# A graph network on one core: the attention's first gathers wait for older TensorE steps, and the last early chunk comes in two halves

## The chip, the cores and the metric

The kernel runs on one core of a Trainium2 chip. The time is device microseconds of one execution, given as the median of several executions; a program on one core has no other core to wait for. The five engines of the core (TensorE or PE, VectorE or DVE, ScalarE or ACT, GpSimd or POOL, SyncE or SP) run their own instruction streams and meet only at semaphores. DMAs are issued here by SP (plain loads and stores) and by POOL (gathers, which read rows of a table in device memory by a list of indices).

## The reference, cut to what matters

Node features are normalised, go through two message-passing convolutions over 200,000 edges and an attention over the same edges, and are added to the input. There are 6,250 nodes of 128 features; edges are sorted by destination.

```python
def mesh_conv(x, src, dst, ea, w1, b1, g, bt, w2, b2):
    m = concatenate([x[dst], x[src], ea], axis=-1) @ w1 + b1
    m = silu(group_norm(m, g, bt))
    m = m @ w2 + b2
    out = segment_sum(m, dst, num_segments=n)
    cnt = segment_sum(ones, dst, num_segments=n)
    return out / clip(cnt, 1.0)[:, None]

h = relu(layernorm(x))                                  # h0
h = silu(group_norm(mesh_conv(h, ...c1), n1_g, n1_b))
h = h + (silu(t_emb) @ tm_w + tm_b)
h = silu(group_norm(mesh_conv(h, ...c2), n2_g, n2_b)) + h0
q, k, v = h @ qw + qb, h @ kw + kb, h @ vw + vb         # 8 heads of 16
logits = (q[dst] * k[src]).sum(-1) * scale + (edge_attr @ ew + eb)
pe = exp(logits - segment_max(logits, dst)[dst])
w = pe / clip(segment_sum(pe, dst)[dst], 1e-06)
o = segment_sum(w[:, :, None] * v[src], dst) @ ow + ob
out = x + h + group_norm(o, an_g, an_b)
```

## The kernel before

**Chunks.** The edges are cut into 1,563 tiles of 128, and 8 tiles make a chunk (`TPC = 8`), so that there are 196 chunks (`NCH`). Chunk number c stands for j = 195 - c: the list is walked from its end. The last chunk, c = 195, has only 3 tiles. Each of three stages (convolution 1, convolution 2, attention) walks all 196 chunks.

**Gathers.** For each tile of a chunk one indirect DMA on POOL (L796, in `gather`) fetches the 128 rows that the edges' sources name: from `b_d` (128 numbers a row) in a convolution, from `kv_d` (k and v, 256 numbers a row) in the attention. The destination's part of the message needs no gather: it is a matmul of a one-hot matrix `ohT` with a window `pk` of a table (L1252 in a convolution, L1521 `qe` in the attention; this matmul is the chunk's "product"). Every gather is ordered behind the one before it (`follows`, `kept.behind`), so POOL runs them in one line: chunk 0, 1, 2, ... of one stage, then of the next.

**Early chunks.** A table is complete only when the stage before it has worked out its last node tile. So that POOL need not stand still there, the first three chunks of convolution 2 and of the attention (`EARLY = 3`) are gathered while the stage before still runs, from copies of the tables, `b_e` and `kv_e`, in which the rows of that last tile are zero. What is missing is added later by a matmul of a one-hot `ohS` with the last tile's rows, `late` (in the attention: `complete`, L1700 and L1702). From chunk 3 on the full tables are read. In the last steps of a stage `pipeline` calls `following.prefetch(c)` for c = 0, 1, 2 of the next stage.

**Buffers.** The gathered rows of chunk c stand in buffer c mod 4 in a convolution and in c mod 11 (`G + 3`) in the attention: `ge0` to `ge2` for the early chunks, `g3` to `g9`, and `gl`. The buffers g3 to g9 use memory that the convolutions had.

**Steps.** `pipeline` (L896 on) is one loop over steps n for each stage. In the attention, step n fetches chunk n + 2 (loads on SP, gathers on POOL); then, where chunks are due, adds up weighted values of older chunks (`second`, L1602); then the logits of chunk n (`first`, L1536 to L1542); in the steps that end a run, the running maxima over the run (`maxima`: two transposes on PE and two scans on DVE, L1565 to L1581); then the one-hot of chunk n + 2 on ACT (`compared`, L763 and L764) and, last, the product of chunk n + 1 on PE. Runs are 4 chunks first (0 to 3), then 8 (4 to 11, 12 to 19, ...), and at the end shorter. Chunks 0 to 3 are weighted and summed in steps 5 to 8, chunks 4 to 11 in steps 13 to 20; steps 9 to 12 have no such work. A chunk's buffer is free when its values have been weighted (`weighted`, L1595), which is done at the end of the step before its sums. On DVE, ACT, PE and SP the instructions run in the order in which the program issues them (`in_order`); POOL's gathers keep their own line.

**The hold.** Before the fetch in step n, `kept.seen` is set to the name of the last PE instruction issued so far (`last_product`), and the first gather of the chunk gets a dependency on it (`held`). In the attention that is mostly the product of chunk n, so the gathers of chunk c may not start before the product of chunk c - 2 is done. The first fetch in the loop of a stage is free of it (`fetched`); in the attention that fetch is chunk 2's, which has its gathers already, and in convolution 1 it is chunk 2's as well. Prefetches of the next stage are held in the same way. `go_on` issues pieces of the node work (batches of four node tiles, once their edges are all summed), which have PE instructions of their own; `last_product` can name one of these.

**The end of a stage.** After the loop `flush` adds the last sums, and `last_tile` (L1187 on) works through the last node tile, with `nodes_of` as a generator: in convolution 2 it stores k and v of that tile into `kv_d` (L1080) and a copy of the node features into `h2_d` (L1105).

Of the kernel before, what the change touches and what calls it, by code (L numbers as in the profile page):

```python
# [31 lines left out]
TPC = 8  # L32
# [6 lines left out]
EARLY = 3  # L39
# [18 lines left out]
def kernel(ctx: ExitStack, tc: tile.TileContext, x, src, dst, eat, w, out):  # L58
# [12 lines left out]
    NCH = -(-EI // TPC)  # L71
# [16 lines left out]
    kept = SimpleNamespace(h0=hpc.tile([P, NW, D], FP, name="h0"))  # L88
# [80 lines left out]
    b_d = {i: dram.tile([NW * P, D], FP, name=f"b_d{i}") for i in (1, 2)}  # L169
    kv_d = dram.tile([NW * P, KV], FP, name="kv_d")  # L170
    b_e = dram.tile([NW * P, D], FP, name="b_e")
    kv_e = dram.tile([NW * P, KV], FP, name="kv_e")
# [72 lines left out]
    with tc.tile_pool(name="node0", bufs=1) as np_, tc.tile_pool(name="prep", bufs=1) as pp, \  # L245
# [99 lines left out]
        back, firsts = sums[:, :NCH], sums[:, 2 * P:2 * P + NCH]  # L345
# [79 lines left out]
    def steps_of(i):  # L425


        ends, due, n = {}, {}, 0
        for m in spread(i):
            ends[n + m] = list(range(n, n + m))  # L430
            due.setdefault(n + m + (i == 3 or n < NCH - SOON), []).extend(ends[n + m])
            n += m
        waiting, todo, left = [], [], NCH
        while left:
            n = len(todo)
            waiting += due.get(n, ())
            steps = min([m for m in due if m > n], default=n + 1) - n
            k = -(-len(waiting) // steps)
            todo.append(waiting[:k])
            waiting = waiting[k:]  # L440
            left -= k
        return ends, todo
# [318 lines left out]
    def compared(k):  # L761

        nc.scalar.activation(k.ohT[:WN, :], k.rel, AF.Square, bias=minus_p[:WN])  # L763
        nc.scalar.activation(k.ohT[:WN, :], k.ohT[:WN, :], AF.Relu, bias=1.0, scale=-4.0)  # L764
# [26 lines left out]
            tc.add_to_no_dep_group(key, h.ins)  # L791

    def gather(k, g, table_d, ring=None):
        n = k.nt
        for t in range(n):
            h = nc.gpsimd.indirect_dma_start(  # L796
                out=g[:, t, :table_d.shape[1]], out_offset=None, in_=table_d,
                in_offset=bass.IndirectOffsetOnAxis(ap=k.src[:, t:t + 1], axis=0))
            if ring is None:
                continue  # L800
            if kept.behind is not None:
                follows(h, kept.behind)
            kept.behind = h.ins
            if t == 0 and kept.seen is not None:
                held(h, kept.seen)
            ring.mark(h, k.at, t, n - 1)

    kept.behind = kept.seen = None

    def last_product():  # L810
        return next((i.name for i in reversed(nc.cur_bb.bb.instructions) if i.engine == mybir.EngineType.PE), None)

    def held(h, name):
        tc.add_manual_dep(
            h.ins, name, mybir.DependencyInfo(mybir.DependencyClass.Sync, mybir.DependencyReason.DATA),
            reason="held until TensorE is there")

    def follows(h, behind):
        tc.add_manual_dep(
            h.ins, behind.name,  # L820
            mybir.DependencyInfo(mybir.DependencyClass.NoSync, mybir.DependencyReason.DATA),
            reason="behind the gathers")
        return h
# [69 lines left out]
    def pipeline(i, stage, following=None, aside=iter(()), then=iter(())):  # L893


        ends, todo = steps_of(i)  # L896
        starts = {n: j for j, (n, _, _) in enumerate(plans[i])}
        ahead = stage.ahead
        ks, under_way, said, fetched = stage.ks, [], {}, False

        def go_on(n, those):
            for g in those:
                if said.get(g) == "held" and n + 1 in ends:
                    continue
                said[g] = next(g, STOP)
                if said[g] is STOP:
                    under_way.remove(g)

        for c in range(ahead):
            if c not in ks:  # L910
                ks[c] = stage.fetch(c)
                compared(ks[c])
        stage.products(ks[0])
        for n, seconds in enumerate(todo):
            new = None
            if n + ahead < NCH and n + ahead not in ks:
                kept.seen = last_product() if fetched else None
                new = ks[n + ahead] = stage.fetch(n + ahead)
                kept.seen, fetched = None, True
            elif following and n + ahead >= NCH:  # L920
                kept.seen = last_product()
                new = following.prefetch(n + ahead - NCH)
                kept.seen = None
            if n + 1 < NCH and stage.soon:
                stage.products(ks[n + 1])
            run = [ks[c] for c in ends.get(n, ())]
            stage.root(run)
            early = stage.soon and n > NCH - SOON
            if early:
                ahead_of = [g for g in under_way if said.get(g) not in ("var", "root")]  # L930
                go_on(n, ahead_of)
            if new and stage.soon:
                compared(new)
            first = (lambda k: lambda: stage.first(k))(ks[n]) if n < NCH else None
            stage.then = [ks[c] for c in (todo[n + 1] if n + 1 < len(todo) else ()) if c in ks]
            if stage.second(run, [ks.pop(c) for c in seconds], first) and first:
                first()
            stage.finish()
            if new and not stage.soon:
                compared(new)  # L940
            if n + 1 < NCH and not stage.soon:
                stage.products(ks[n + 1])
            if n + 1 < len(todo):
                stage.early(ks, n, todo[n + 1])
            if n in starts:
                for _ in aside:
                    pass
                under_way.append(stage.batch(starts[n]))
            go_on(n, [g for g in under_way if not early or g not in ahead_of])
            if n > 4 and next(aside, STOP) is STOP and n > min(starts):  # L950
                next(then, None)
            if n < NCH:
                stage.reduce(ks[n])
        stage.flush()
        for g in (*under_way, aside, then):
            for _ in g:
                pass
# [206 lines left out]
    def nodes_of(b, i, w, m, hx=None):  # L1164
        return attention_nodes(b, w, m, hx) if i == 3 else conv_nodes(b, i, w, m, last=hx is not None)
# [22 lines left out]
    def last_tile(b, i, hx=True):  # L1188

        slots, b.bank = b.bank(), None  # L1190
        turn = itertools.cycle(range(BN))

        def slot():
            j = next(turn)
            return slots[:, j:j + 1, :]

        b.bank = slot
        b.var = lambda: last_var
        b.rs = last_rs
        nc.scalar.activation(last_sd[:, :1], eps_t, AF.Sqrt)  # L1200
        for r in nodes_of(b, i, 0, 1, hx):
            if r == "root":
                nc.scalar.activation(last_sd, last_var, AF.Sqrt, bias=eps_t, scale=1.0 / HD)  # L1203
            if r == ("inverse" if i == 3 else "root"):
                nc.vector.reciprocal(last_rs, last_sd)  # L1205
# [10 lines left out]
    def convs(general=False):  # L1216
        with ExitStack() as es:
            pool = lambda n, b, **kw: es.enter_context(tc.tile_pool(name=f"{n}{'g' if general else 'c'}", bufs=b, **kw))
            pools = {"oh": pool("oh", 2), "ps": pool("ps", 1, space=PSUM)}
            if not general:  # L1220
                pools["ohT"] = pool("ohT", 2)
                ring = Ring("ring", GB)
# [75 lines left out]

            class Stage:
                ahead, soon = 2, True  # L1300

                def __init__(self, i):
                    self.i, self.ks = i, {}
                    self.sums, self.late, self.roots, self.next = [], [], False, 0
                    self.var, self.j, self.sd = None, 0, None
                    self.wins = Numbers(w0_i, DVE, NW - 1)
                    self.pools = {"low": Numbers(lo_i, SP, N - 1), "ohT": pools["ohT"]}
# [6 lines left out]
                def fetch(self, c):  # L1314
                    k = chunk(self.i, c)
                    loads(k, self.pools, a_d[self.i], wc_d[self.i])
                    k.g = gp.tile([P, TPC, D], FP, name="g")
                    gather(k, k.g, b_d[self.i] if k.ohS is None else b_e, ring)
                    k.h = hs[c % len(hs)]
                    return k  # L1320

# [144 lines left out]
    gs = [None] * (G + 3)  # L1466

    class AheadOfAttention:

        @staticmethod  # L1470
        def prefetch(c):
            k = chunk(3, c)
            gather(k, gs[c], kv_e, ring3)

    ahead_of = AheadOfAttention()

    def attention(general=False):
# [197 lines left out]

        class Stage:
            ahead, soon = 2, False
            sums, late, nb = [], [], None
            lg, j, both = None, 0, None

# [128 lines left out]
        if not general:  # L1809
            stage = Stage()  # L1810
# [49 lines left out]
    ring3 = Ring("ring3", G + 3)  # L1860
# [30 lines left out]
    with tc.tile_pool(name="lastn", bufs=1) as lp, tc.tile_pool(name="lastp", bufs=1, space=PSUM) as ps:  # L1891
        hx = [lp.tile([P, 1, D], FP, name=f"hx{j}") for j in range(2)]
# [45 lines left out]
```

## Time and profile before

| | |
|---|---|
| median of 3 runs | 6007.2 us (6005.33 to 6008.46) |
| profiled execution | 6010.35 us, of which 6008.6 us is the span from its first to its last instruction |
| indirect gathers | 3102 `g<-b_d`, 24 `g<-b_e`, 24 `ge<-kv_e`, 995 `g<-kv_d`, 408 `ge<-kv_d`, 136 `gl<-kv_d` |
| granted PE clock, mean | 0.746 of full speed |

The profile is of one execution. Times are microseconds from the first instruction. In the rows of the timeline stand the start, the duration, the engine, the line of the kernel, the operation, the tile written and the tiles read, how many instructions are merged, and in brackets how long the engine had been idle and what released it ("issue": nothing that the profile can name). For a gather on POOL the duration is that of the instruction on POOL; its rows land later. PEld is PE's weight load, SPq an instruction on SP's queue, POOLq one on POOL's.

### The profile page before, as it was taken

How to read it: one execution, taken by the hardware profiler on the slowest of the kernel's cores; microseconds unless marked ns; L12 is line 12 of the kernel's file. 1: busy time of each engine (PE TensorE's matmuls, PEld its weight loads, DVE VectorE, ACT ScalarE, POOL GpSimd, SP SyncE). 2: the span in 40 equal slices, each digit the busy share in tenths (PEclk: the TensorE clock that was granted, in tenths of full speed). 3: DMA queues.
4: the chain of work that ended last, by engine and by line, in shares of the span. 5: the costliest groups of instructions: out<-in, count | busy, mean ns of one | idle time of the engine just before them, and what ended most of it. 6: DMA issues, size and time to landing. Idle time of an engine off the chain costs nothing. (4 is left out here: it accounts for less than half of the span.)

```text
span 6008.6 us, 66534 instructions
## 1 busy us (share of the span) xinstructions
PE 3651.7 (61%) x20680; PEld 3461.7 (58%) x20681; DVE 4879.3 (81%) x6840; ACT 3324.6 (55%) x5207; POOL 4503.0 (75%) x4763
## 2 busy tenths in 40 slices
PE   6665555555555665555566655555666666666665
PEld 5555555555555555555555555555666565666565
DVE  7888888888888777777888888856787788888876
ACT  5666666666666666666666666642333333333574
POOL 7777777777777777777777777767777777777775
PEclk7667777777777777777777777867777777777777
DMA  5333333333333323233333333334444455555553
GB/s 158 90 108 100 80 87 89 91 92 89 91 92 88 81 78 81 78 82 78 83 98 99 100 98 102 102 86 137 137 135 136 135 140 144 142 147 138 147 143 84
DMA packets 384005, 640.81 MB, mean 107 GB/s; under 512 B 91184, under 2 KB 249628, under 8 KB 382059
## 3 DMA queue, kind: packets, MB, share of 16 engines
q0 software_dynamic: 175056, 410.03, 25.9%
q1 hardware_dynamic: 205482, 225.32, 13.1%
q8 instruction: 167, 2.74, 0.2%
q14 instruction: 196, 1.61, 0.1%
q10 hardware_dynamic: 3104, 1.12, 0.1%
HBM read 588.95 MB, written 47.17 MB: 106 GB/s over the span
## 5 line engine op out<-in xcount | busy, mean ns | idle before, releaser
L796 POOL DMA_INDIRECT g<-b_d,src_i x3102 | 2944.8, 949 | 951.6 <-issue 924.7
L1291 PE MATMUL u<-h,oh 128*128 128x129 f32 (+1 forms) x6252 | 1330.0, 399 | 1514.5 <-ACT h L1283 1514.5
L1291 PEld LDWEIGHTS u<-h,oh 128*128 128x128 f32 x6252 | 1229.3, 302 | 1590.9 <-ACT h L1283 1590.9
L796 POOL DMA_INDIRECT g<-kv_d,src_i x995 | 944.5, 949 | 333.9 <-issue 311.9
L1252 PE MATMUL m<-pk,ohT 101*128 101x128 f32 x6252 | 918.9, 309 | 63.7 <-DVE h L1259 44.3
L1252 PEld LDWEIGHTS m<-pk,ohT 101*128 101x128 f32 x6252 | 898.1, 228 | 75.7 <-DVE h L1259 53.7
L1259 DVE TENSOR_TENSOR h<-m,g 128x1024 f32<-128x1024 f32 x392 | 475.9, 1214 | 570.7 <-DMA g<-b_d,src_i 535.1
L1521 PE MATMUL qe<-pk,ohT 101*128 101x136 f32 x3126 | 595.6, 365 | 349.2 <-ACT ebs L1538 341.3
L1602 PE MATMUL us<-v,oh 128*128 128x145 f32 x3126 | 610.3, 366 | 294.1 <-DVE flat L1627 206.7
L1521 PEld LDWEIGHTS qe<-pk,ohT 101*128 101x128 f32 x3126 | 551.4, 263 | 383.9 <-ACT ebs L1538 375.5
L1602 PEld LDWEIGHTS us<-v,oh 128*128 128x128 f32 x3126 | 564.9, 256 | 337.4 <-DVE flat L1627 160.9
L1261 ACT ACTIVATE sq<-h 128x1024 f32<-128x1024 f32 x392 | 412.8, 1053 | 569.4 <-DVE h L1259 567.8
L1283 ACT ACTIVATE h<-h 128x1024 f32<-128x1024 f32 (+2 forms) x394 | 413.2, 1049 | 558.9 <-DVE h L1282 543.1
L763 ACT ACTIVATE ohT<-rel,minus_p 96x1024 f32<-96x1024 bf16 x588 | 668.7, 1137 | 16.8 <-DMA rel<-rel_d 8.6
L764 ACT ACTIVATE ohT<-ohT 96x1024 f32<-96x1024 f32 x588 | 619.9, 1054 | 19.2
L1263 DVE TENSOR_REDUCE var<-sq 128x64 f32<-128x1024 f32 x392 | 473.9, 1209 | 25.5 <-ACT sq L1261 25.1
L1281 DVE TENSOR_TENSOR h<-h,cps 128x1024 f32<-128x1024 f32 (+2 forms) x394 | 477.4, 1212 | 13.5
L1282 DVE TENSOR_TENSOR h<-h,cps 128x1024 f32<-128x1024 f32 (+2 forms) x394 | 477.4, 1212 | 13.5
L796 POOL DMA_INDIRECT ge<-kv_d,src_i x408 | 388.6, 952 | 124.3 <-issue 119.4
L1278 DVE TENSOR_TENSOR h<-h,cps 128x1024 f32<-128x1024 f32 (+2 forms) x394 | 474.5, 1204 | 0.8
L827 DVE TENSOR_TENSOR oh<-cps,dm 128x1024 f32<-128x1024 f32 x392 | 474.3, 1210 | 0.7 <-PE u L1291 0.6
L1615 ACT ACTIVATE us<-d 128x16 f32<-128x16 f32 x172 | 32.1, 187 | 602.6 <-DVE d L1611 435.2
(294 smaller groups left out, 4459.9 us busy)
## 6 DMA issues: line engine op xcount, KB each, us to landing
rel<-rel_d SPq DMA_DIRECT2D x291, 384.0 KB
g<-b_d,src_i POOLq DMA_INDIRECT x3102, 2.6
pk<-a_d SPq DMA_DIRECT2D x588, 46.0 KB
g<-kv_d,src_i POOLq DMA_INDIRECT x995, 2.8
ohT<-in_eat_dram SPq DMA_DIRECT2D x291, 40.0 KB
ge<-kv_d,src_i POOLq DMA_INDIRECT x408, 2.8
a_d<-n_o SPq DMA_DIRECT2D x24, 256.0 KB
kv_d<-n_o SPq DMA_DIRECT2D x24, 256.0 KB
```

Source lines behind the costliest of these rows:

```text
L763: nc.scalar.activation(k.ohT[:WN, :], k.rel, AF.Square, bias=minus_p[:WN])
L764: nc.scalar.activation(k.ohT[:WN, :], k.ohT[:WN, :], AF.Relu, bias=1.0, scale=-4.0)
L796: h = nc.gpsimd.indirect_dma_start(out=g[:, t, :table_d.shape[1]], out_offset=None, in_=table_d, in_offset=bass.IndirectOffsetOnAxis(ap=k. ...
L827: return nc.vector.tensor_tensor(k.oh[:, :k.nt, :], iota[:, None, :].to_broadcast([P, k.nt, P]), k.dm[:, :, None].to_broadcast([P, k.nt, P ...
L1252: nc.tensor.matmul(k.m[:, t, :], lhsT=lhs[:, t * P:(t + 1) * P], rhs=rhs, start=(j == 0), stop=(j == len(terms) - 1))
L1259: nc.vector.tensor_tensor(k.mt, k.m[:, :n], k.g[:, :n], ALU.add)
L1278: nc.vector.tensor_tensor(m4, m4, k.rs.rearrange("p (t g) -> p t g", g=H)[:, a:a + n, :, None].to_broadcast([P, n, H, HD]), ALU.mult)
L1281: nc.vector.tensor_tensor(mt, mt, over_edges(gam, n), ALU.mult)
L1282: nc.vector.tensor_tensor(mt, mt, over_edges(bet, n), ALU.add)
L1291: nc.tensor.matmul(k.u[:, 0, :wide(k)], lhsT=k.oh[:, t, :], rhs=k.h[:, t, :wide(k)], start=start and t == 0, stop=stop and t == k.nt - 1)
L1521: nc.tensor.matmul(k.qe[:, t // TB, at:at + DB], lhsT=lhs[:, t * P:(t + 1) * P], rhs=rhs, start=(j == 0), stop=(j == len(terms) - 1))
L1602: nc.tensor.matmul(k.u[:, :wide], lhsT=k.oh[:, t, :], rhs=k.v[:, t, :wide], start=(t == 0), stop=(t == k.nt - 1))
```

## The change

`gather` becomes a loop over a generator, `gathered`, which can stop before tile 0 and tile 4 (`halves`) and then holds the gather behind the last PE instruction issued at that moment. `early_gather` issues the gathers of an early chunk; for chunk 2 it issues none yet. Chunk 2's first four gathers are issued at the end of `pipeline`, before `flush`, and its last four in `last_tile`, after the seventh piece of the last node tile (behind the transposition of its normalised values).

In `pipeline` a list `marks` holds, for each step, the last PE instruction at the step's begin, taken before `go_on` issued pieces of node batches (`kept.mark`). The gathers of chunk c = n + 2 are held behind `marks[n - lag(c)]`, and only for c > 3 and where the index isn't negative. `lag` is 0 in the convolutions; in the attention it is 3 below chunk 12, 2 below 14, 1 below 19 and for the last chunk, else 0.

```diff
     def gather(k, g, table_d, ring=None):
+        for _ in gathered(k, g, table_d, ring):
+            pass
+
+    def gathered(k, g, table_d, ring, halves=False):
+
         n = k.nt
         for t in range(n):
+            if halves and t % (TPC // 2) == 0:
+                yield
+                kept.seen = last_product()
             h = nc.gpsimd.indirect_dma_start(
...
-            if t == 0 and kept.seen is not None:
+            if (t == 0 or halves) and kept.seen is not None:
                 held(h, kept.seen)
+                kept.seen = None
             ring.mark(h, k.at, t, n - 1)
-
-    kept.behind = kept.seen = None
+        yield
+
+    def early_gather(c, *what):
+        kept.rest = gathered(*what, c == EARLY - 1)
+        next(kept.rest)
+
+    kept.behind = kept.seen = kept.rest = kept.mark = None
...
-        ks, under_way, said, fetched = stage.ks, [], {}, False
+        ks, under_way, said, marks = stage.ks, [], {}, []
+        kept.mark = None
...
         for n, seconds in enumerate(todo):
             new = None
+            marks.append(kept.mark or last_product())
             if n + ahead < NCH and n + ahead not in ks:
-                kept.seen = last_product() if fetched else None
+                back = n - stage.lag(n + ahead)
+                kept.seen = marks[back] if n + ahead > EARLY and back >= 0 else None
                 new = ks[n + ahead] = stage.fetch(n + ahead)
-                kept.seen, fetched = None, True
+                kept.seen = None
...
                 under_way.append(stage.batch(starts[n]))
+            kept.mark = last_product()
             go_on(n, [g for g in under_way if not early or g not in ahead_of])
...
                 stage.reduce(ks[n])
+        if following:
+            next(kept.rest)
         stage.flush()
...
-        for r in nodes_of(b, i, 0, 1, hx):
+        for n, r in enumerate(nodes_of(b, i, 0, 1, hx)):
+            if i < 3 and n == 6:
+                next(kept.rest)
...
             class Stage:
                 ahead, soon = 2, True
+                lag = staticmethod(lambda c: 0)
...
-                    gather(k, k.g, b_d[self.i] if k.ohS is None else b_e, ring)
+                    if k.ohS is None:
+                        gather(k, k.g, b_d[self.i], ring)
+                    else:
+                        early_gather(c, k, k.g, b_e, ring)
...
-            gather(k, gs[c], kv_e, ring3)
+            early_gather(c, k, gs[c], kv_e, ring3)
...
         class Stage:
             ahead, soon = 2, False
+            lag = staticmethod(lambda c: 3 if c < 12 else 2 if c < 14 else 1 if c < 19 or c == NCH - 1 else 0)
```

## The prediction

> **What bounds the kernel.** I read the page first: it says which engine has the least room, and how its busiest group spends its time.
>
> ```profile
> span 6008.6 us, 66534 instructions
> PE 3651.7 (61%) x20680; PEld 3461.7 (58%) x20681; DVE 4879.3 (81%) x6840; ACT 3324.6 (55%) x5207; POOL 4503.0 (75%) x4763
> L796 POOL DMA_INDIRECT g<-b_d,src_i x3102 | 2944.8, 949 | 951.6 <-issue 924.7
> L796 POOL DMA_INDIRECT g<-kv_d,src_i x995 | 944.5, 949 | 333.9 <-issue 311.9
> ```
>
> DVE has the larger busy share, yet POOL is the bound. A gather takes 949 ns, and for convolution gathers the idle time before one is 951.6 / 3102 = 0.31 us on the mean, put down to nothing that is waited for: that is POOL's own spacing, and a gather costs 1.25 us in all. In the attention the first group has 333.9 / 995 = 0.34. The excess stands in a few places, and POOL's timeline has them: I went through it from end to end, and these five rows are all the gathers behind the first one that were idle for more than 0.4 us before. (Between them stand rows that I need below.)
>
> ```profile
> 72.69 0.94 POOL L796 DMA_INDIRECT g<-b_d,src_i  x1 [1.05 <-PE m L1252]
> ...
> 3980.97 0.95 POOL L796 DMA_INDIRECT ge<-kv_e,src_i  x1 [0.30 <-issue]
> ...
> 3985.97 0.95 POOL L796 DMA_INDIRECT ge<-kv_e,src_i  x1 [0.30 <-issue]
> ...
> 3989.72 0.95 POOL L796 DMA_INDIRECT ge<-kv_e,src_i  x1 [0.30 <-issue]
> 4011.50 0.94 POOL L796 DMA_INDIRECT g<-kv_d,src_i  x1 [20.84 <-issue]
> ...
> 4024.36 0.94 POOL L796 DMA_INDIRECT g<-kv_d,src_i  x1 [3.16 <-PE qe L1521]
> ...
> 4038.15 0.94 POOL L796 DMA_INDIRECT g<-kv_d,src_i  x1 [4.09 <-issue]
> ...
> 4048.15 0.95 POOL L796 DMA_INDIRECT g<-kv_d,src_i  x1 [0.30 <-issue]
> ...
> 4138.12 0.94 POOL L796 DMA_INDIRECT g<-kv_d,src_i  x1 [0.30 <-issue]
> ...
> 5949.05 0.94 POOL L796 DMA_INDIRECT g<-kv_d,src_i  x1 [3.90 <-PE qe L1521]
> ```
>
> The rows at 4011.50, 4024.36, 4038.15 and 4048.15 are the first gathers of the attention's chunks 3, 4, 5 and 6; 72 gathers on, 4138.12 is chunk 15's, so a chunk takes (4138.12 - 4048.15) / 9 = 10.00 us. What ended three of the holes, PE's rows say:
>
> ```profile
> 4006.74 4.00 PE L1521 MATMUL qe<-pk,ohT 101*128 101x136 f32 x16 [3.00 <-ACT ebs L1538]
> 4020.09 4.00 PE L1521 MATMUL qe<-pk,ohT 101*128 101x136 f32 x16 [3.00 <-ACT ebs L1538]
> 4033.60 3.79 PE L1521 MATMUL qe<-pk,ohT 101*128 101x136 f32 x16 [3.00 <-ACT ebs L1538]
> 4039.13 2.61 PE L1521 MATMUL qe<-pk,ohT 101*128 101x136 f32 x16 [1.74 <-ACT ebs L1538]
> ```
>
> The first three are the products of chunks 1, 2 and 3; they end at 4010.74, 4024.09 and 4037.39, and the gathers of chunks 3, 4 and 5 start 0.76, 0.27 and 0.76 us later. So the hold on the product of chunk c - 2 is what ends last in each hole, the unnamed ("issue") ones too. The compute there is slow because each early chunk must first be completed. From chunk 6 on, but for the last chunk, the hold is met before POOL arrives.
>
> **The change, part by part.**
>
> *Holes in the attention's start.* Chunks 3 and 4 lose the hold (3 is not above EARLY, and for 4 the index is -1). What else chunk 3 needs is the last tile's k and v, and memory that the convolution used:
>
> ```profile
> 3970.94 5.00 PE L1291 MATMUL u<-h,oh 128*128 128x128 f32 x22 [7.22 <-ACT h L1283]
> 3979.90 0.47 PE L972 MATMUL nd<-ident,n_A 128*128 128x128 f32 x1 [1.23 <-DVE n_A L1001]
> 3983.06 1.56 SPq L1080 DMA_DIRECT2D kv_d<-late  x2
> 3986.25 0.33 SPq L1105 DMA_DIRECT2D h_d<-n_x  x1
> 3987.22 0.33 SPq L725 DMA_DIRECT2D rel<-rel_d  x1
> 3991.38 1.15 ACT L763 ACTIVATE ohT<-rel,minus_p 96x1024 f32<-96x1024 bf16 x1 [5.15 <-DMA rel<-rel_d]
> ```
>
> The stores into `kv_d` are out by 3984.62, and the convolution's last store, of `n_x`, goes out at 3986.25. How long a store takes no row says. From below it is nothing; from above I take the far larger load of `rel`, issued at 3987.22 and used at 3991.38, 4.16 us. Then the last store has landed by 3990.41. POOL is done with chunk 2 at 3989.72 + 0.95 + 0.30 = 3990.97, so either end hides it, and chunk 3 follows without a hole, 20.54 us earlier than now (20.84 less the 0.30 of spacing). Chunk 4 and chunk 5 follow at 4000.97 and 4010.97; chunk 5 is held on the product of chunk 0, which PE ran before that of chunk 1, done at 4010.74 at the latest. So the holes of 3.16 and 4.09 go too, 2.86 and 3.79. Chunk 6 (4020.97) waits for product 1 (4010.74), 7 (4030.97) for 2 (4024.09), 8 (4040.97) for 3 (4037.39), 9 (4050.97) for 4 (4041.74): all met, by 3.6 us at the least.
>
> *Convolution 1's chunk 3* loses its hold as well: the row at 72.69, 1.05 - 0.30 = 0.75 us. POOL has no hole between there and 3990, so this goes through.
>
> *The last chunk* is held a step earlier: 3.90 - 0.30 = 3.60 us of POOL. I count it as nothing; the tail's rows below are why.
>
> *Chunk 2 in halves* moves eight gathers in POOL's order past nothing: they stay behind chunk 1 and ahead of chunk 3. They gain two waits. The first half follows the last product of the loop, done at 3970.94 + 5.00 = 3975.94, against 3980.97 where POOL gets there; the second half follows the transposition at 3979.90, done at 3980.37, against 3985.97. Both are met 5 us early. In the change from convolution 1 to 2 the order is the same and the cover is:
>
> ```profile
> 2021.35 0.47 PE L972 MATMUL nd<-ident,n_A 128*128 128x128 f32 x1 [2.00 <-DVE n_A L1001]
> 2027.78 0.94 POOL L796 DMA_INDIRECT g<-b_e,src_i  x1 [0.30 <-issue]
> ```
>
> 2021.82 against 2027.78, 6 us. Were the cover gone, chunk 3 and every gather behind it would be late by the difference. Queued behind on POOL is only the next gather; SP, which issues the stores, is not touched.
>
> *Older marks* elsewhere can only be met earlier. But an older mark may cover less, and a gather may then need a semaphore wait of its own:
>
> ```profile
> L796 POOLq EVENT_SEMAPHORE  x596: 17/43/24205, 31.8 to 5936.2; - x199
> ```
>
> Such instructions stand there now, about one for each of the 588 chunks with a median of 43 ns, and the first gathers of chunks 6 and 15 still show 0.30 of idle time, like any other. So POOL's queue gets them done while the gather before runs. Bounds: nothing, or the full 43 ns for each chunk, 25 us; I take nothing, by these two rows, and keep the other end as a rival.
>
> *Does the compute follow?* POOL 27 us ahead needs free buffers. Buffers 3 to 10 are filled at once, 11 to 14 take those of chunks 0 to 3; the narrow one is chunk 15, which takes chunk 4's and needs its values weighted, behind the first run of 8.
>
> ```profile
> 4069.79 1.29 DVE L1536 TENSOR_TENSOR g<-qe,g 128x768 f32<-128x768 f32 x2 [1.01 <-DMA g<-kv_d,src_i]
> ...
> 4079.96 1.29 DVE L1536 TENSOR_TENSOR g<-qe,g 128x768 f32<-128x768 f32 x2 [3.69 <-DMA g<-kv_d,src_i]
> ...
> 4109.74 1.29 DVE L1536 TENSOR_TENSOR ge<-qe,ge 128x768 f32<-128x768 f32 x2 [7.11 <-DMA ge<-kv_d,src_i]
> ...
> 4111.44 3.99 PE L1521 MATMUL qe<-pk,ohT 101*128 101x136 f32 x16 [5.99 <-ACT ebs L1538]
> ...
> 4119.81 1.29 DVE L1536 TENSOR_TENSOR ge<-qe,ge 128x768 f32<-128x768 f32 x2 [7.20 <-DMA ge<-kv_d,src_i]
> ...
> 4130.13 1.22 DVE L1595 TENSOR_TENSOR v<-g,pe 128x1024 f32<-128x1024 f32 x1 [0.38 <-ACT v L1591]
> ```
>
> These are the logits of chunks 7, 8, 11 and 12 and the weighting of chunk 4. DVE waits for gathers already at chunk 7: the compute has caught up there. Without the waits of 1.01 and 3.69, chunk 8's logits start at 4075.26. The next four steps have no sums. Each then needs its logits, the copy, and the next product: from 4109.74 to 4111.44 + 3.99 = 4115.43, with 0.1 for the release 5.8 us. Chunk 12's logits start at 4075.26 + 4 x 5.8 = 4098.5, and chunk 4 is weighted 4131.35 - 4119.81 = 11.54 later, at 4110.0. POOL comes to chunk 15 at 3990.97 + 12 x 10.00 = 4110.97. It fits by 0.9 us, so this costs nothing; with one microsecond more per step it would cost about 4. Behind it a step moves on faster than a chunk's gather, and once chunk 19 the relations are those of now, earlier by the whole gain.
>
> The product's time decides how narrow that is: 3.99 behind 5.99 of idle time, 2.61 behind 1.74. [...]
>
> *The tail.*
>
> ```profile
> 5796.05 1.29 DVE L1536 TENSOR_TENSOR g<-qe,g 128x768 f32<-128x768 f32 x2 [1.48 <-DMA g<-kv_d,src_i]
> ...
> 5973.52 0.51 DVE L1536 TENSOR_TENSOR g<-qe,g 128x384 f32<-128x384 f32 x1
> ```
>
> The first row is the last logits that waited for a gather; from there on the compute runs by itself. That wait ties the tail to POOL: what POOL gains by then, the end gains. The last chunk's logits run at 5973.52, 24 us behind its gathers' start at 5949.05, so its 3.60 us buys nothing.
>
> **Sum.** 20.54 + 2.86 + 3.79 + 0.75 = 27.94 us. The profiled execution took 6010.35, 1.75 around its span, and is 3.15 above the median of 6007.2; it would become 5982.4, and the median 5979.3.
>
> **The rivals.**
>
> *Another wait takes the first hole's place.* Chunk 3 would wait for something of the attention's start that the 20.84 us hide now. For it: the row names nothing, and what holds it is inferred from 4010.74. Against: nothing of the convolution is open past 3990.41. If the hole stays whole, the gain is 27.94 - 20.54 = 7.4, 5999.8; a half of it gives 5989.5. Chance 0.09.
>
> *The catch-up fails.* The completing steps or the four short ones run slower beside gathers that POOL now issues there, or chunk 15 comes too early, and POOL stands. Against: the gathers from 4011.50 on ran beside the same kind of step without a longer product. At 2 us a step, 8 us lost: 5987. Chance 0.09.
>
> *Waits that are not hidden: the other side.* If older marks cost every chunk two waits of 43 ns that POOL can't overlap, 588 x 0.086 = 50.6 us are added and 27.9 gained: 6029.9. It decides from 27.94 / 588 = 0.048 us a chunk. Against stand the 0.30 of 4048.15 and 4138.12. Chance 0.04.
>
> *The tail gains too.* If the last chunk's gathers, or the one-hots behind them on POOL, are on the path, up to 3.60 more: 5975.7. For it, the hole is real; against, the 24 us above. Chance 0.07.
>
> **How the numbers follow.** The forecast has 0.70; 0.01 is left for what I don't see. A difference of 0.2%, 12 us, is what a measurement of this kernel tells from no change: 5995.2 and 6019.2 are the limits. Faster are the forecast, the failed catch-up, the tail and about half of the first rival, 0.70 + 0.09 + 0.07 + 0.04, with half of the rest 0.90; the same, the other half of the first rival and a single unhidden wait (25 us), 0.06; slower, 0.04. The range: below, 27.94 + 3.60 and the scatter of the runs (6005.33 is 1.9 under the median) give 5973.8, a little under it 5972; above, the failed catch-up and a hole closed by a third (27.94 - 13.7 = 14.2, 5993) lie within 5995.
>
> **What would show it.** In the changed profile: chunk 3's first gather at about 3990 with 0.30 before it, the holes of chunks 4 and 5 and the one at 72.69 gone, chunk 15 without a hole at about 4110, the last gather's start near 5917 and the last waiting logits near 5768; a gather still 0.30 behind the one before. DVE's waits for gathers in chunks 7 to 11 should shrink and be back by chunk 19. Wrong is the prediction if a hole over 1 us stands at chunk 3 or at 15, or if the spacing grows.

## The result, and the profile after

The changed kernel took 5977.53 us in the median of 5 runs (5975.87 to 5978.94), against 6007.3 us for the kernel before in 5 runs beside it (6005.33 to 6008.91). The ratio is 0.9951, with a 95% interval of 0.9938 to 0.9964: faster by 29.8 us, where 27.9 were forecast. The profiled execution took 5977.53 us, of which 5975.8 is its span; 6010.35 and 6008.6 were those of before.

The page of the changed kernel, its span, the busy times and POOL's two large groups of gathers (L804 is the line that was L796; behind the count stand busy time, mean ns, and the idle time ahead of them):

```profile
span 5975.8 us, 66535 instructions
PE 3631.2 (61%) x20680; PEld 3439.3 (58%) x20681; DVE 4877.1 (82%) x6840; ACT 3323.4 (56%) x5207; POOL 4500.1 (75%) x4763
L804 POOL DMA_INDIRECT g<-b_d,src_i x3102 | 2942.3, 949 | 951.0 <-issue 921.5
L804 POOL DMA_INDIRECT g<-kv_d,src_i x995 | 944.2, 949 | 303.1 <-issue 286.6
```

Every engine runs as many instructions as before, and a gather takes 949 ns as before. What is gone is idle time of POOL: ahead of the attention's gathers 333.9 - 303.1 = 30.8 us, and 303.1 / 995 = 0.30 is now the mean, the bare spacing. (These 30.8 us include 3.60 ahead of the last chunk.) The convolutions lose only 0.6 us.

POOL's timeline of the changed kernel, the rows that answer to the five holes of before: the first gather of all, the first of convolution 1's chunk 3, the last early gather, the first of the attention's chunks 3, 4, 5 and 15, the first of the last chunk, and the last of all.

```profile
38.96 1.17 POOL L804 DMA_INDIRECT g<-b_d,src_i  x1 [5.86 <-issue]
...
70.98 0.94 POOL L804 DMA_INDIRECT g<-b_d,src_i  x1 [0.30 <-issue]
...
3985.52 0.95 POOL L804 DMA_INDIRECT ge<-kv_e,src_i  x1 [0.30 <-issue]
3986.77 0.95 POOL L804 DMA_INDIRECT g<-kv_d,src_i  x1 [0.30 <-issue]
...
3996.75 0.95 POOL L804 DMA_INDIRECT g<-kv_d,src_i  x1 [0.31 <-issue]
...
4006.74 0.94 POOL L804 DMA_INDIRECT g<-kv_d,src_i  x1 [0.30 <-issue]
...
4106.70 0.95 POOL L804 DMA_INDIRECT g<-kv_d,src_i  x1 [0.30 <-issue]
...
5913.54 0.97 POOL L804 DMA_INDIRECT g<-kv_d,src_i  x1 [0.30 <-DVE l L1566]
...
5916.06 0.95 POOL L804 DMA_INDIRECT g<-kv_d,src_i  x1 [0.30 <-issue]
```

Behind the first, no gather of this kernel was idle for more than 0.4 us before it. Chunk 3 follows the last early gather by 1.25 us, where it was 21.78 (3989.72 to 4011.50). From chunk 3 to chunk 15 it is 4106.70 - 3986.77 = 119.93 us, 12 chunks at 9.99, so no stall took the place of the old ones.

The products `qe` on PE (L1547, L1521 before) of chunks 1, 3, 10 and 11, and that of chunk 13 with the transposition ahead of it:

```profile
4002.50 4.00 PE L1547 MATMUL qe<-pk,ohT 101*128 101x136 f32 x16 [3.00 <-ACT ebs L1564]
...
4027.75 2.12 PE L1547 MATMUL qe<-pk,ohT 101*128 101x136 f32 x16 [3.00 <-ACT ebs L1564]
...
4074.19 2.12 PE L1547 MATMUL qe<-pk,ohT 101*128 101x136 f32 x16 [1.74 <-ACT ebs L1564]
4078.05 2.12 PE L1547 MATMUL qe<-pk,ohT 101*128 101x136 f32 x16 [1.74 <-ACT ebs L1564]
...
4097.43 1.08 PE L1600 MATMUL blk<-ident,fw 64*128 64x64 f32 x8 [12.52 <-DVE fw L1596]
4098.44 3.99 PE L1547 MATMUL qe<-pk,ohT 101*128 101x136 f32 x16
```

The product of chunk 1 ends at 4006.50, 19.7 us after chunk 3's first gather has started: POOL no longer follows PE. And DVE's side, the logits (L1562) of chunks 9 to 12, the weighting of chunk 4 (L1621), the last logits that waited for a gather, and those of the last chunk:

```profile
4072.49 1.29 DVE L1562 TENSOR_TENSOR g<-qe,g 128x768 f32<-128x768 f32 x2 [2.08 <-PE qe L1547]
4076.35 1.29 DVE L1562 TENSOR_TENSOR gl<-qe,gl 128x768 f32<-128x768 f32 x2 [0.99 <-PE qe L1547]
4080.21 1.29 DVE L1562 TENSOR_TENSOR ge<-qe,ge 128x768 f32<-128x768 f32 x2 [0.99 <-PE qe L1547]
4089.91 1.29 DVE L1562 TENSOR_TENSOR ge<-qe,ge 128x768 f32<-128x768 f32 x2 [6.82 <-DMA ge<-kv_d,src_i]
4100.21 1.22 DVE L1621 TENSOR_TENSOR v<-g,pe 128x1024 f32<-128x1024 f32 x1 [0.37 <-ACT v L1617]
...
5764.56 1.29 DVE L1562 TENSOR_TENSOR g<-qe,g 128x768 f32<-128x768 f32 x2 [1.73 <-DMA g<-kv_d,src_i]
...
5939.90 0.51 DVE L1562 TENSOR_TENSOR g<-qe,g 128x384 f32<-128x384 f32 x1
```

Chunks 7 to 11 waited for gathers before; now chunks 9 to 11 wait for the product, and at chunk 12 DVE waits for a gather again (6.82 us). The compute is behind POOL up to chunk 11 and then has caught up. The last waiting logits stand at 5764.56, 31.49 us earlier than at 5796.05.

### The profile page after: what moved, and what is told of

The parts are those of the page before. It is cut to its first block, busy times and chain, and to the rows that moved or that the text cites. A ratio compares the mean times of both kernels' runs of the same rounds, so it can differ in the third digit from the quotient of the medians.

```text
span 5975.8 us, 66535 instructions
## 1 busy us (share of the span) xinstructions
PE 3631.2 (61%) x20680; PEld 3439.3 (58%) x20681; DVE 4877.1 (82%) x6840; ACT 3323.4 (56%) x5207; POOL 4500.1 (75%) x4763
## 5 line engine op out<-in xcount | busy, mean ns | idle before, releaser
L804 POOL DMA_INDIRECT g<-b_d,src_i x3102 | 2942.3, 949 | 951.0 <-issue 921.5
L804 POOL DMA_INDIRECT g<-kv_d,src_i x995 | 944.2, 949 | 303.1 <-issue 286.6
L1547 PE MATMUL qe<-pk,ohT 101*128 101x136 f32 x3126 | 581.1, 358 | 327.1 <-ACT ebs L1564 318.9
L1547 PEld LDWEIGHTS qe<-pk,ohT 101*128 101x128 f32 x3126 | 537.0, 257 | 361.9 <-ACT ebs L1564 353.8
L804 POOL DMA_INDIRECT ge<-kv_d,src_i x408 | 388.4, 952 | 124.3 <-issue 116.7
```

Source lines behind the costliest of these rows:

```text
L804: h = nc.gpsimd.indirect_dma_start(out=g[:, t, :table_d.shape[1]], out_offset=None, in_=table_d, in_offset=bass.IndirectOffsetOnAxis(ap=k. ...
L1547: nc.tensor.matmul(k.qe[:, t // TB, at:at + DB], lhsT=lhs[:, t * P:(t + 1) * P], rhs=rhs, start=(j == 0), stop=(j == len(terms) - 1))
```

## The experiments

The theory to test: the lags in the attention's start carry the gain, because POOL bounds the kernel from there on; halves, older marks elsewhere and the last chunk are worth nothing. All kernels but one were made from the changed kernel by the edit shown.

### Four doses of lag, on a chip where the kernel before takes 16% longer

The first is lags of 0 in the attention, but for the last chunk.

```diff
-            lag = staticmethod(lambda c: 3 if c < 12 else 2 if c < 14 else 1 if c < 19 or c == NCH - 1 else 0)
+            lag = staticmethod(lambda c: 1 if c == NCH - 1 else 0)
```

> All of the change but the lag: in the attention chunk 4 and later are again held on the product of chunk c - 2 (the last chunk keeps its lag of 1), chunk 3 is free. My theory: a hole that is taken away at chunk 3 comes back at chunk 4, for POOL gets there at 3996.8 and product 2 is done at about 4019.7 (clock of the changed kernel's trace), a hole of some 23 us; chunk 6 then starts within 1 us of where it started before, and the time is 6004 to 6007, no gain but the 0.75 of convolution 1 and what the start varies. Rival (dropping the first hold is what counts, the other holds were only late because the first was): 20.5 us gained, about 5986.

The second is a lag of 1 up to chunk 18.

```diff
+            lag = staticmethod(lambda c: 1 if c < 19 or c == NCH - 1 else 0)
```

> As the changed kernel, with a lag of 1 instead of 3 and 2 for chunks below 14. My theory: chunk 4 waits for product 1 (done at 4006.5, POOL there at 3996.8: a hole of about 10), chunk 5 for product 2 (4019.7 against 4016.9: about 3), chunk 6 for product 3 (about even): 13 us lost against the changed kernel, 5991. Rival as for the lag of 0: 5978 to 5980, since the first hold is gone.

The third is 2 up to chunk 13 and then 1.

```diff
+            lag = staticmethod(lambda c: 2 if c < 14 else 1 if c < 19 or c == NCH - 1 else 0)
```

> As the changed kernel, with a lag of 2 instead of 3 for chunks below 12. My theory: chunk 5 on product 1 about even (4006.5 against 4006.8), chunk 6 on product 2 (4019.7 against 4016.8, with the release about 3.5 lost), chunk 7 on product 3 even: 3 to 5 us lost against the changed kernel, 5981 to 5982.5. Rival: nothing lost.

The fourth has no hold on a step anywhere in the attention: the index into the marks is always negative.

```diff
+            lag = staticmethod(lambda c: NCH)
```

> As the changed kernel, with no hold at all for the attention's fetches: every gather has only the waits that its buffer needs. My theory: the holds are met before POOL gets there and a wait instruction on POOL's queue lies beside the gather before, so the time is that of the changed kernel, 5977.5 within 2 us, with 0.30 us between all gathers. Rival (a gather without a hold needs semaphore waits of its own, which POOL can't overlap): 196 chunks by 43 to 86 ns, 8 to 17 us slower than the changed kernel, 5986 to 5994; or holes where a buffer is waited for in a worse way.

Measured: 6963.73, 6975.80, 6963.38 and 7434.79 us. But the kernel before took 6968.59 us there, 16% more than on the other chips, so the ratios are 0.9991 (0.9983 to 1.0000), 1.0009 (1.0001 to 1.0018), 0.9992 (0.9983 to 1.0001) and 1.0661 (1.0646 to 1.0677). None came out as expected. What is different there, the waits of PE show, here from 1000 to 2000 us, in the middle of the convolutions, which no edit touches (waiting operation, releaser, sum, times, longest). First the changed kernel, on its own chip:

```profile
PE u L1313 <- ACT h L1305: 392.8, 101, 7.0
PE m L1274 <- DVE h L1281: 15.9, 17, 1.7
```

Then the kernel with lags of 0, on this chip:

```profile
PE u L1313 <- issue: 196.5, 78, 10.1
PE m L1274 <- issue: 124.9, 105, 3.2
PE u L1313 <- ACT h L1305: 101.3, 33, 8.3
```

On its own chip PE waits almost only for ACT. Here it stands for 196.5 + 124.9 us in that millisecond while nothing that the profile can name holds it. A gather on POOL takes as long as in the changed kernel (in the median 944 ns in the convolutions and 946 in the attention, in both), while PE's product `m` takes 325 ns on the mean in that millisecond where it is 299, at a granted clock of 0.70 instead of 0.77. POOL isn't the bound there: with lags of 0, 352 of the 4,689 gathers were idle for more than 0.4 us before them, 1,114 us in all, and in the changed kernel on its own chip it is only the first. Taking three holes away then moves nothing clear, and the three times don't follow the dose (a lag of 1 is the slowest): these runs are no test of the theory, and they show where its condition ends. The fourth was slower than any of its expectations; it was run again below.

### The lags alone

The kernel before, with the lags of the attention and nothing else of the change: no halves, marks as before, conv 1's chunk 3 and the last chunk held as before.

```diff
-        ks, under_way, said, fetched = stage.ks, [], {}, False
+        ks, under_way, said, fetched, marks = stage.ks, [], {}, False, []
...
+            marks.append(last_product())
             if n + ahead < NCH and n + ahead not in ks:
-                kept.seen = last_product() if fetched else None
+                c = n + ahead
+                back = n - (0 if i < 3 else 3 if c < 12 else 2 if c < 14 else 1 if c < 19 else 0)
+                kept.seen = marks[back] if fetched and back >= 0 and not (i == 3 and c <= EARLY) else None
```

> The kernel before with the attention's lags alone (3, 2, 1, 0, and no hold for chunks 3 and 4): chunk 2 is gathered whole where it was, marks are taken where they were (they can name pieces of node batches), convolution 1's third chunk keeps its hold, the last chunk its hole. My theory: the three holes of the attention's start are all that counts, so 27.2 of the 27.9 us are gained and the time is within 2 us of the changed kernel's, 5978 to 5980. Rival (the halves or the earlier marks are needed, since chunk 3 would otherwise find a wait in place of its hold): a hole over 1 us at chunk 3 and up to 20 us less gain, 5980 to 5999.

Measured: 5978.85 us (5975.73 to 5981.41) beside 6004.41 for the kernel before; ratio 0.9956 (0.9943 to 0.9970). The changed kernel's ratio, 0.9951, lies inside this interval. In POOL's timeline two holes are left behind the first gather, those of the two holds that this kernel keeps:

```profile
72.82 0.94 POOL L796 DMA_INDIRECT g<-b_d,src_i  x1 [2.46 <-PE m L1255]
...
5918.44 0.94 POOL L796 DMA_INDIRECT g<-kv_d,src_i  x1 [2.63 <-PE qe L1524]
```

So the gain is that of the lags; halves, earlier marks and the last chunk's hold are worth less than these runs can tell.

### Extra work on POOL, early, late and last

If POOL bounds the attention, work put on POOL there must cost its full length. 17 one-hots were written into a tile that nothing reads, ahead of the gathers of one chunk: 40, 188 or the last, 195.

```diff
+    idle = const.tile([P, P], FP, name="idle")
...
+                if c == 40:        # 188 in the second kernel, NCH - 1 in the third
+                    for _ in range(17):
+                        h = nc.gpsimd.tensor_scalar(idle, iota_j, k.dm[:, 0:1], None, ALU.is_equal)
+                        kept.behind = follows(h, kept.behind).ins
```

> The changed kernel with 17 extra instructions on POOL (one-hots of 128 x 128 into a tile that nobody reads, 0.58 us each, 9.9 us in all) ahead of the gathers of the attention's chunk 40. My theory: POOL sets the time from 39 us on to the last logits that wait for a gather (5764.6), so the end moves by all of it: 10 us slower than the changed kernel, about 5987.5. Rival (DVE, busy 82%, is what bounds the attention, and the gain came from an earlier start of its work): under 3 us slower.

> The same 9.9 us of POOL work ahead of the gathers of chunk 188, in the tail. My theory: behind 5764.6 the compute runs by itself and the gathers are ahead of it, so these 10 us are hidden: within 2 us of the changed kernel, 5977.5, and the last chunk's lag (3.6 us of POOL in the tail) is worth nothing in the same way. Rival (the tail is on POOL too): up to 10 us slower.

> 17 extra one-hots of 0.6 us on POOL, about 12.2 us from first to last as measured ahead of chunk 188, now ahead of the last chunk's gathers in the changed kernel. The changed kernel's last logits start at 5939.90, its last gather is issued at 5916.06 and lands some 2.6 us after its end, so the last chunk has some 20 us of slack, and the prediction counted the hole of 3.6 us there as nothing for that. My theory expects the extra work hidden: within 3 us of the changed kernel, or up to 5 more through POOL's own one-hots at 5924.72, which come behind it. Rival (POOL bounds the kernel to its end): 12 us above the changed kernel, with the last logits waiting for their gather.

*Early*: 5990.22 us (5987.36 to 5993.73), on the same chip as the lags alone and 11.4 above them. POOL's timeline has the price:

```profile
4356.20 0.94 POOL L805 DMA_INDIRECT g<-kv_d,src_i  x1 [0.30 <-issue]
4357.18 11.82 POOL L1720 TENSOR_SCALAR idle<-iota_j,dm 128x128 f32<-128x128 f32 x17
4369.16 1.03 POOL L805 DMA_INDIRECT g<-kv_d,src_i  x1 [0.16 <-issue]
```

From gather to gather it is 12.96 us where it is 1.25 elsewhere, 11.71 more, and the two spans differ by 5988.8 - 5977.1 = 11.7. The lags alone are not quite this kernel (they keep two holds). The next kernel, the same as this one up to chunk 188 and on the same chip, is the closer one to compare with: its last waiting logits stand at 5766.76, here they stand at 5777.91, 11.15 later. To within a microsecond the full length shows: POOL is the bound.

*Late*: 5986.00 us (5983.28 to 5987.90), 7.2 above the lags alone. I had expected it hidden. DVE's rows, the logits of chunks 187 to 189:

```profile
5857.03 1.28 DVE L1563 TENSOR_TENSOR ge<-qe,ge 128x768 f32<-128x768 f32 x2
5870.27 1.29 DVE L1563 TENSOR_TENSOR ge<-qe,ge 128x768 f32<-128x768 f32 x2 [4.41 <-DMA ge<-kv_d,src_i]
5879.97 1.29 DVE L1563 TENSOR_TENSOR ge<-qe,ge 128x768 f32<-128x768 f32 x2 [3.96 <-DMA ge<-kv_d,src_i]
```

Two new waits, 4.41 + 3.96 = 8.37 us. The gathers came 12.1 us later (5857.86 instead of 1.25 behind 5844.52), so some 7.7 us of it were slack at chunk 188; at chunk 189, whose gathers come as much later, the slack was only 12.1 - 8.37 = 3.7. "The last logits that waited" at 5764.56 doesn't mean that everything behind it runs free by a wide margin: a few us later, and the gathers set the pace again.

```profile
5844.52 0.95 POOL L805 DMA_INDIRECT ge<-kv_d,src_i  x1 [0.30 <-issue]
5845.51 12.20 POOL L1720 TENSOR_SCALAR idle<-iota_j,dm 128x128 f32<-128x128 f32 x17
5857.86 1.03 POOL L805 DMA_INDIRECT ge<-kv_d,src_i  x1 [0.16 <-issue]
```

*Last*: 5977.92 us (5977.15 to 5979.08), beside 6004.04 for the kernel before; ratio 0.9955 (0.9941 to 0.9968). No cost shows. On POOL and on DVE:

```profile
5915.49 11.73 POOL L1720 TENSOR_SCALAR idle<-iota_j,dm 128x128 f32<-128x128 f32 x17
5927.38 1.03 POOL L805 DMA_INDIRECT g<-kv_d,src_i  x1 [0.16 <-issue]
...
5930.95 20.27 POOL L1700 TENSOR_SCALAR oh<-iota_j,dm 128x128 f32<-128x128 f32 x35
```

```profile
5942.31 0.51 DVE L1563 TENSOR_TENSOR g<-qe,g 128x384 f32<-128x384 f32 x1
```

The last chunk's first gather starts 11.6 us later than POOL could have had it (5927.38 against 5915.75, which is 1.25 behind the gather at 5914.50), its logits run without a wait for it, and the span is 5975.9, where the changed kernel on its own chip has 5975.8. So a hole of 3.6 us ahead of this chunk costs nothing either.

### The doses again, where the kernel before takes 6004 us

Three of the four doses, beside the kernel with POOL's extra work last. The lag of 2 was not run again.

> The changed kernel with lags of 0 for every attention chunk but the last: the first gathers wait for the newest TensorE step, as before the change, while halves and earlier marks stay. Repeated because the first run of it fell on a chip on which the kernel before itself took 6968.59 us and TensorE was short of instructions all through, so that gathers set nothing there. Where the kernel before takes about 6005: my theory (the lags carry the gain) expects the holes of 20.8, 2.9 and 3.8 us ahead of attention chunks 3 to 5 back and 6002 to 6008 us, no more than 3 us under the kernel before. Rival (halves and earlier marks carry a good part): at or under 5992.

> A lag of 1 instead of 3 and 2 for chunks 3 to 13, 1 up to chunk 18 as in the changed kernel. My theory (each gather start follows its mark's product, and what POOL gains at chunk 3 stays only if compute is caught up when the hold is back) expects a part of the hole back: 5988 to 5996 us where the kernel before takes about 6005, and holes ahead of chunks 3 to 5 that sum to 10 to 15 us. Rival (one step of distance is enough, the first two steps of lag buy nothing more): within 3 us of the changed kernel's distance, about 27 us under the kernel before.

> No hold on a TensorE step for any attention chunk; only buffers that come free and loaded indices hold the gathers. It was 6.6% slower than the kernel before on the chip where TensorE was short of instructions, which my theory hadn't foreseen. My theory now: that loss belongs to that chip, and on one where the kernel before takes about 6005 the gathers stand back to back either way, so 5974 to 5981 us, within 4 us of the changed kernel. Rival (the steady hold keeps gathers from crowding other transfers or instruction fetches on every chip): over 6100 us, with idle time of DVE, ACT and TensorE that no engine of the trace ended.

The kernel before took 6004.04 us there.

| lag of the first chunks | us (lowest to highest) | ratio (95% interval) |
|---|---|---|
| 0 | 6004.85 (5995.52 to 6008.10) | 0.9999 (0.9990 to 1.0008) |
| 1 | 5993.37 (5989.95 to 5995.98) | 0.9980 (0.9971 to 0.9989) |
| no hold at all | 5979.21 (5976.80 to 5982.45) | 0.9957 (0.9944 to 0.9971) |
| 3, then 2, then 1 (the change, with the extra work last) | 5977.92 (5977.15 to 5979.08) | 0.9955 (0.9941 to 0.9968) |

With lags of 0, POOL's timeline:

```profile
4022.16 0.94 POOL L804 DMA_INDIRECT g<-kv_d,src_i  x1 [24.45 <-PE qe L1547]
...
4035.95 0.94 POOL L804 DMA_INDIRECT g<-kv_d,src_i  x1 [4.08 <-issue]
```

and the products of chunks 2 and 3 in the same kernel:

```profile
4017.90 3.99 PE L1547 MATMUL qe<-pk,ohT 101*128 101x136 f32 x16 [3.00 <-ACT ebs L1564]
...
4031.39 3.79 PE L1547 MATMUL qe<-pk,ohT 101*128 101x136 f32 x16 [3.00 <-ACT ebs L1564]
```

These are chunks 4 and 5. Chunk 3 has lost its hold in this kernel too and runs at once, but chunk 4 then stands until product 2 is done (4021.89, and 4022.16 is 0.27 later), and the sum of the holes, 24.15 + 3.78 = 27.93 without the spacing, is the 27.19 of the attention's three holes before and the 0.75 that POOL has gained in convolution 1 and now waits longer. Freeing chunk 3 alone moves the hole by one chunk; what counts is when the last held chunk of the start may go. With a lag of 1:

```profile
4007.63 0.94 POOL L804 DMA_INDIRECT g<-kv_d,src_i  x1 [10.49 <-PE qe L1547]
...
4021.48 0.94 POOL L804 DMA_INDIRECT g<-kv_d,src_i  x1 [4.16 <-issue]
...
4034.30 0.94 POOL L804 DMA_INDIRECT g<-kv_d,src_i  x1 [3.13 <-PE qe L1547]
```

10.19 + 3.86 + 2.83 = 16.88 us of holes are left, for chunks 4, 5 and 6 behind the products of 1, 2 and 3. For chunks 3 to 5 I had expected 10 to 15, and it is 14.05; the 2.83 at chunk 6 I had not expected. The times above the change on the same chip are 26.9 us for lag 0 (holes 27.93) and 15.5 for lag 1 (holes 16.88): what stands in POOL's line is what the end pays, within 1.5 us. The granted clock doesn't explain these times: its mean over the profiled run is 0.753 with a lag of 1, 0.751 with no hold and 0.750 with the change. And no hold at all is the change again, 1.3 us apart: POOL's spacing in that kernel is the bare one,

```profile
L804 POOL DMA_INDIRECT g<-kv_d,src_i x995 | 943.6, 948 | 303.1 <-issue 290.0 <-DVE us L1651 2.1 <-DVE d L1638 1.8
```

so the 6.6% that it lost in its first run doesn't come from the program alone. It was seen on that chip only and on one occasion, and the runs don't tell the one from the other.

## Why the prediction was right

**The bound.** POOL's line of gathers, and not DVE with its 81%: shown by the extra work at chunk 40, which cost its full length, 11.7 us, to within a microsecond.

**The attention's holes.** Forecast 20.54 + 2.86 + 3.79 = 27.19 us between the last early gather and the last waiting logits. Measured: the last early gather came 3989.72 - 3985.52 = 4.20 earlier, the last waiting logits 31.49, and the difference is 27.29. The hold was what ended all three holes, the one without a name too: with lags of 0 they come back as one of 24.15 and one of 3.78, 0.27 and 0.77 us behind a product's end, as in the trace of before. The first rival, another wait in chunk 3's place, is refuted by the 0.30 at 3986.77.

**Convolution 1's chunk 3** gave its 0.75: from the first gather to the last early one it was 3985.52 - 38.96 = 3946.56 us, and before, by the row below, 3989.72 - 39.95 = 3949.77, which is 3.21 less. The other 2.46 is gathers that were shorter in this execution (2942.3 against 2944.8 us busy in the group of convolution gathers). The 0.75 is small only because the first gather of that trace came late: where the hold was kept, chunk 3 started at 72.69 (before) and 72.82 (the lags alone, first gather at 38.88, a hole of 2.46), and without the hold it starts at 70.98.

```profile
39.95 1.17 POOL L796 DMA_INDIRECT g<-b_d,src_i  x1 [5.75 <-DMA a_d<-a]
```

**Halves and marks** cost nothing, as forecast: 0.30 stands ahead of every early gather and ahead of chunk 3. They gain nothing either that shows beside the lags alone. The rival on the other side, two unhidden waits a chunk, is refuted by the 0.30 that stands everywhere.

**The catch-up** had more room than forecast, and this is the step whose size was off. I took the slow product, 3.99 us, a step of 5.8 us, and a margin of 0.9 at chunk 15. The logits of chunks 9, 10 and 11 start at 4072.49, 4076.35 and 4080.21, 3.86 us apart; chunk 4 is weighted at 4101.43, and chunk 15's first gather goes out at 4106.70, a margin of 5.3. Against POOL, which is 4.27 us earlier at chunk 15 than in the forecast, chunk 12's logits came 4.3 us early (4089.91 + 4.27 = 4094.18, forecast 4098.5), and that is all of the gain in margin: the end of chunk 4's weighting follows them by 11.52 us, where I took 11.54. They would have come earlier still, but waited 6.82 us for their own gather, so the margin that is left is set by the gathers' pace and no longer by the product. The product took 2.12 us in these steps, with 1.74 us of idle time ahead of each; behind 12.52 us of idle time and 1.08 of other work, at 4098.44, it takes 3.99. My 3.99 came from a row behind 5.99 us of waiting for a gather, and I used it for a stretch in which, up to chunk 11, nothing waits for gathers any more.

The idle time alone doesn't tell which time the product takes: behind 3.00 us the product of chunk 1 takes 4.00 and that of chunk 3 takes 2.12. The granted clock goes with the two times: in this trace it is 0.50 over the products of chunks 1 and 13, and 1.00 over those of chunks 3 and 10; in the trace of before it is 0.50 over the 3.99 at 4111.44 and 0.78 over the 2.61 at 4039.13. What sets it, no run here shows.

**The tail.** The conclusion held, and the reason was partly wrong. The last chunk's hole is worth nothing: 11.6 us of delay there cost nothing. But the step "from there on the compute runs by itself" is too strong: 12.1 us at chunk 188 put back 8.37 us of waits. The slack doesn't grow steadily: it is none at 5764.56, some 7.7 us at chunk 188, 3.7 at chunk 189 and over 11 at the last chunk.

**The size.** Forecast for the profiled execution was a span of 6008.6 - 27.94 = 5980.7; it was 5975.8, 4.9 less. The parts are 0.99 from the first gather (38.96 against 39.95), the 2.46 of shorter gathers, and 1.31 in the tail (5975.8 - 5764.56 = 211.24 against 6008.6 - 5796.05 = 212.55). None of them was forecast. The first gather started between 38.35 and 39.36 in the seven runs from the lags alone on, that kernel's too, so the 0.99 lies in the one trace of before and not in the change; with the hold on convolution 1's chunk 3 it would have gained nothing. The shorter gathers are not the change's: the changed kernel with the extra work last has gathers of 2944.6 us in the convolutions, as the kernel before, and takes 5977.92.

```profile
L805 POOL DMA_INDIRECT g<-b_d,src_i x3102 | 2944.6, 949 | 950.9 <-issue 927.4 <-DMA b_d<-b 5.9 <-DVE h L1305 5.5
```

In the later runs the kernel before took 6004.41 and 6004.04 us, and the distance is 25.6 (the lags alone) and 26.1 (the change with the extra work last). The forecast 27.9 lies between these and the 29.8. The runs don't settle it closer than that, and a closer match would have been luck.

## What to carry to other kernels

An engine that issues transfers in one line may be the bound at a busy share of 75%, as here with a gap of 0.30 us behind each gather of 0.95; look then for the few gaps that exceed it, add them up, and take each away whole, since freeing one item of the line only moves the gap to the next that is held (with lags of 0, 24.15 us ahead of chunk 4). Extra work put on that line at a few places shows where it bounds the end, and how much slack there is at each. When a chain that had waited for others is let run, cost its steps by rows of a dense stretch (here 3.86 us a step) and not by those behind a wait (5.8, as forecast).

## What was not expected of the hardware

One of the chips ran the kernel before in 6968.59 us where the others took 6004 to 6007. Granted clocks are somewhat lower there (0.695 in the run with lags of 0, 0.747 in its repeat), gathers are as long (944 and 946 ns in the median), PE's products `m` are 9% longer (325 ns against 299), and PE has idle times of up to 10.1 us that nothing in the profile ended. (Expectations above say that TensorE was short of instructions there; the traces show these idle times, and not what PE lacked.) On that chip the unheld attention was 6.6% slower than the kernel before (7434.79 against 6968.59 us), and on another 0.4% faster (5979.21 against 6004.04), by the same program. The window from 5000 to 5700 us, in the attention of both, with the columns PE, PEld, DVE, ACT and POOL busy (and instructions), granted clock, DMA share and GB/s, for the unheld kernel there:

```profile
5000.00:5700.00 700.00, 323.12 (x1678) 293.07 (x1677) 390.43 (x810) 155.14 (x444) 375.37 (x396) 0.67 0.36 96
```

and for the same program on the later chip:

```profile
5000.00:5700.00 700.00, 446.82 (x2501) 415.15 (x2500) 602.30 (x1260) 288.34 (x780) 530.35 (x557) 0.76 0.51 145
```

Every engine gets through 29 to 43% fewer instructions, and the DMA engines are busy for 0.36 of the time where it is 0.51, so a fuller DMA is not what is seen. What ends PE's idle times, and why the kernel whose gathers run ahead loses more there, no run here tells; it stays open. From lags of 0 to no hold the time rose by 471.06 us there (6963.73 to 7434.79), and on the later chip it fell by 25.64 (6004.85 to 5979.21): what a hold is worth differed that much between the two.
